# Graph products of an attention kernel gathered in one block: order of products, denominators and keys

## The chip, the cores and the metric

The kernel runs on one core of one Trainium2 chip. The metric is the device time of one execution in microseconds; three runs of the kernel before took 2455.43, 2456.01 and 2456.99 us, median 2456.01. Below, PE is the matmul engine, ACT the engine for activations and copies, DVE the vector engine, POOL the second, slower vector engine, SP the engine whose queue issues most DMAs. L1066 is line 1066 of the kernel before.

## The reference

Two layers over x (16 batches of 1024 nodes with 256 features, float32), each followed by a residual sum and a layernorm. The change touches the first layer only:

```python
c_adj = jnp.mean(fea, axis=1)                       # fea = x transposed, (B, C, N)
diff = c_adj[:, None, :] - c_adj[:, :, None]
A = jnp.abs(jnp.abs(jax.nn.sigmoid(diff) - 0.5) - 0.5) * 2.0
Wg = adj[None, :, :] * ((A + jnp.transpose(A, (0, 2, 1))) * 0.5)
g = jax.nn.relu(jnp.einsum('bcn,bnm->bcm', fea, Wg) * para.reshape(1, C, N))
q = ...   # g, cut into 4 heads of 64
k, v = ...  # x @ kv_w, cut likewise
out = jnp.einsum('bhnm,bhmd->bhnd', softmax(jnp.einsum('bhnd,bhmd->bhnm', q, k) * scale), v)
x = _layernorm(x + out)
```

The second layer multiplies with a normalised adjacency, then two linear maps with batchnorms, a residual and a layernorm.

## The kernel before, in words

**Stages.** The first layer runs batch by batch until about 1600 us of the span; the second layer follows in two passes over all batches. The first layer's instructions on PE, ACT, DVE and SP stand in exactly the order in which the program writes them (a manual schedule); POOL's follow in order as well. Buffers come from small pools: a tile takes a free buffer of its tag, and its first writer waits until the last reader of the buffer's former tile is done.

**Bursts.** The attention of a batch has 32 units: 2 pairs of heads, 2 halves of the queries, 8 chunks of the keys. Two units make a burst, 16 bursts (u = 0 to 15) make a batch. For a unit `scores` multiplies keys and queries into a PSUM tile of 1024 columns (`ps`, L1066, two buffers of tag "s"), and ACT takes the exponential into `p` (L1071, four buffers). `outputs` multiplies `p` with the values (`po`, L1087, two buffers of tag "o") and DVE adds `p` up into `acc` (L1095, L1097), the softmax's denominators still spread over partitions. In each turn of the loop PE gets the scores of burst j, then the outputs of burst j-1, and then whatever else stands at that u. When a half of the queries is complete, ACT and DVE bring the output out of PSUM (L1104, L1105), DVE transposes it in squares of 32 and SP sends it through memory (L1115, L1116, L1125).

**What else stands at which burst.** While batch b is attended to, batch b+1 is prepared and batch b-1 is finished:

- u=0: values and keys of batch b+1 (`steps`, seven of the eight, L1006 and L993), weights of its graph (`side`, L838, L843, L847), the denominators of the former batch's second pair (`normalise`, L1134: eight matmul passes with a matrix of ones, a copy `drow` on ACT L1140, four DMAs out and four in).
- u=1: `residual` of that pair (reciprocals L1155, POOL multiplies and adds, L1161 and L1162). u=2 and u=3: halves of the layernorm's statistics of batch b-1 on DVE (L620, L621); after the second, POOL makes the coefficients (L593, L595, L625, L626).
- u=4: two calls from `late`, `finish_x1` (L1180): eight blocks of `t * rstd + nmr` on ACT (L630), and after the second half the store of the result, issued by POOL (L1183).
- u=4 to u=8: the graph product of batch b+1, in seven block products of four accumulating steps each (eight matmul passes, `product`, L896) instead of eight, after Winograd. DVE makes the sums that they need: `left_first`, `left_third`, `left_last` of x (tile `S`), `right(1)` to `right(4)` of the weights (tile `wg`, in place, four subtractions each, L882). Products accumulate in PSUM tiles of tag "t" (two buffers); products 1 and 2 share `pga`, 3 has `pgd`, 6, 7 and 4 share `pgb`, 5 has `pgc`. Results are put together in `qT`, weighed with `para_s` and rectified (`weigh`, `rectify`).
- u=8: `begin` of batch b+2 (its column of means on DVE, L796, and five DMAs that spread it as a row), and `normalise` of the batch's own first pair. u=11: `residual` of that pair.
- u=9 to u=15: x of batch b+2 arrives in squares (L764) and is transposed by DVE (L820, u=12 and u=15); one step of its `side` per burst. In the last batch but one the adjacency's squares (L1249) come in the same places.

The part of the schedule that the change edits is, in the kernel before:

```python
elif u == 4:
    p = st[b + 1]["graph"]["p"]
    keys_last = steps[:1] if b else []
    del steps[: len(keys_last)]
    p[1]()
    run(keys_last, 1)
    run(late, 2)
    p[2]()
    p[3]()
```

Of the kernel before, what the change touches and what calls it, by code (L numbers as in the profile page):

```python
# [10 lines left out]
F32 = mybir.dt.float32  # L11
# [504 lines left out]
def fast_path(  # L516
# [43 lines left out]
    def tile_s(name):  # L560
        return psum["s"].tile([P, N], F32, tag="s", name=name)

    def tile_t(name):
        return psum["t"].tile([P, HALF], F32, tag="t", name=name)

    def tile_o(name):
        return psum["o"].tile([P, HALF], F32, tag="o", name=name)
# [167 lines left out]
    with (  # L735
# [46 lines left out]
        def prologue(b):  # L782
# [77 lines left out]
            KC = range(NCH // 2)  # L860

            def left_first():
                s2, s4 = s["S"][:, 0], s["S"][:, 1]
                nc.vector.tensor_tensor(s2, A21, A22, ALU.add)
                nc.vector.tensor_tensor(s2, s2, A11, ALU.subtract)
                nc.vector.tensor_tensor(s4, A12, s2, ALU.subtract)

            def left_third():
                nc.vector.tensor_tensor(s["S"][:, 1], A11, A21, ALU.subtract)

            def left_last():
                nc.vector.tensor_tensor(s["S"][:, 0], A21, A22, ALU.add)

            def right(k):
                for i in KC:
                    dst, one, two = {
                        1: (lo(i, H1), lo(i, H1), lo(i, H0)),
                        2: (hi(i, H1), hi(i, H1), lo(i, H1)),
                        3: (lo(i, H0), hi(i, H1), lo(i, H0)),
                        4: (hi(i, H0), hi(i, H0), hi(i, H1)),  # L880
                    }[k]
                    nc.vector.tensor_tensor(dst, one, two, ALU.subtract)  # L882
# [18 lines left out]
            def q_at(c, hs):  # L901
                return s["qT"][:, c, hs]

            def rectify(c, hs):
                q = q_at(c, hs)
                nc.scalar.activation(q, q, AF.Relu, scale=-scale)  # L906
# [4 lines left out]

            pg = {}

            def p1():
                s["qT"] = qkv.tile([P, CC, N], F32, tag="qT", name=f"qT_{b}")
                s["S"] = xsp.tile([P, 2, NCH // 2, P], F32, tag="xS", name=f"S_{b}")
                pg["a"] = tile_t(f"pga_{b}")
                product(1, pg["a"], True)
                nc.scalar.copy(q_at(1, H0), pg["a"])  # L919
                left_first()  # L920
                right(1)

            def p3():
                pg["d"] = tile_t(f"pgd_{b}")
                product(3, pg["d"], True)
                nc.scalar.copy(q_at(0, H1), pg["d"])

            def p2():
                product(2, pg["a"], False)
                nc.vector.tensor_mul(q_at(0, H0), pg["a"], para_s[:, 0, H0])  # L930
                rectify(0, H0)

            def between(u):
                right(u - 3)
                if u == 6:
                    nc.vector.tensor_add(q_at(0, H1), q_at(0, H1), q_at(1, H0))
                if u == 7:
                    left_third()

            def p6():  # L940
                pg["b"] = tile_t(f"pgb_{b}")
                product(6, pg["b"], True)
                nc.vector.tensor_add(q_at(0, H1), pg["b"], q_at(0, H1))
                left_last()

            def p7():
                product(7, pg["b"], False)
# [9 lines left out]

            def p4():
                product(4, pg["b"], False)
                nc.vector.tensor_add(q_at(1, H0), pg["b"], q_at(1, H0))  # L960
                weigh(1, H0)

# [78 lines left out]
                )]  # L1041
            if b:
                s["graph"] = dict(
                    between=between, p=(None, p1, p2, p3, p4, p5, p6, p7),
                )
            return first, steps, side

# [79 lines left out]
        def normalise(b, pr):  # L1127


            k = b * PAIRS + pr  # L1130
            last = k == B * PAIRS - 1
            den = tile_s("den_last")[:, H0] if last else tile_t(f"den_{k}")
            for i in range(4):
                nc.tensor.matmul(  # L1134
                    den[i * 32 : (i + 1) * 32, :], ones[:, :32],
                    G[b, pr, i // 2]["acc"][:, (i % 2) * HALF : (i % 2 + 1) * HALF],
                    start=True, stop=True,
                )
            row = rdp.tile([P, HALF], F32, tag="drow", name=f"drow_{k}")
            nc.scalar.copy(row, den)  # L1140
            for i in range(4):
                nc.sync.dma_start(den_d[k][i : i + 1, :], row[i * 32 : i * 32 + 1, :])
            for qh in range(2):
                col = small.tile([P, 4, 2], F32, tag="dcol", name=f"dcol_{k}_{qh}")
                for hd in range(2):
                    i = 2 * qh + hd
                    nc.sync.dma_start(
                        col[:, :, hd], den_d[k][i : i + 1, :].rearrange("o (n p) -> p (o n)", p=P)
                    )
                G[b, pr, qh]["col"] = col  # L1150
# [34 lines left out]
        def run(fs, k):  # L1185
            for f, a in fs[:k]:
                f(*a)
            del fs[:k]
# [135 lines left out]
        with tc.manual_schedule(  # L1324
# [64 lines left out]
            for j in range(len(bursts)):  # L1389
                b, u = j // PERB, j % PERB  # L1390
                for i in bursts[j]:
                    scores(i)
                if u == 0:
                    steps, side = next_steps, next_side
                    next_first, next_steps, next_side = [], [], []
                if j:
                    back(j - 1)
                if u in (5, 9, 13):
                    run(rows_of, 1)
                if u == 5 and b + 2 < B:  # L1400
                    load_x(b + 2)
                    next_first, next_steps, next_side = prologue(b + 2)
                if b == B - 1:
                    if u == 0:
                        run(sums, 1)
                        run(rows_of, 1)
                    elif u in (2, 13):
                        run(full, 2)
                    elif u == 8:
                        run(sums, 1)  # L1410
                    elif u == 3:
                        late.clear()
                elif u == 0:
                    for i in range(7):
                        if b:
                            run(steps, 1)
                            run(side, (2, 3, 2, 3, 2, 2, 99)[i])
                        if i == 1:
                            run(sums, 1)
                            run(rows_of, 1)  # L1420
                elif u < 4:
                    if u == 1:
                        run(full, 2)
                    else:
                        run(late, 1)
                    run(side, 99)
                elif u == 4:
                    p = st[b + 1]["graph"]["p"]
                    keys_last = steps[:1] if b else []
                    del steps[: len(keys_last)]  # L1430
                    p[1]()
                    run(keys_last, 1)
                    run(late, 2)
                    p[2]()
                    p[3]()
                elif u == 8:
                    p = st[b + 1]["graph"]["p"]
                    p[6]()
                    run(next_first, 1)
                    run(sums, 1)  # L1440
                    if b == B - 2:
                        adjacency_diagonal()
                        for n in range(6):
                            adjacency_rows(n)
                    p[7]()
                    p[5]()
                    p[4]()
                elif u < 8:
                    st[b + 1]["graph"]["between"](u)
                else:  # L1450
                    if u == 9 and b + 2 < B:
                        load_squares(b + 2, 0)
                    if u == 11:
                        run(full, 2)
                    if u == 12:
                        run(next_first, 1)
                        if b + 2 < B:
                            load_squares(b + 2, 1)
                    if u == 15:
                        run(next_first, 1)  # L1460
                    run(next_side, 1)
                if b == B - 2:
                    run(before_last.get(u, []), 9)
                if b == B - 1:
                    run(last.get(u, []), 9)
# [591 lines left out]
```

## Time and profile before

| what | value |
|---|---|
| median of three runs | 2456.01 us |
| profiled execution, its own time | 2458.24 us |
| its span, first to last instruction | 2456.5 us |
| PE busy | 2418.9 us, 98% |
| DVE busy | 1863.6 us, 76% |
| ACT busy | 1236.0 us, 50% |
| POOL busy | 478.5 us, 19% |
| mean granted clock of PE | 0.997 |
| one attention batch (281.27 to 377.96) | 96.69 us |

A line of a timeline has the start in us of the span, the length of the piece in us, engine, line, operation, what it writes and reads, shape and count; in brackets stands the idle time of that engine just before, and what ended it. A line of a table by stages has the stretch, its length, the busy time (and instructions) of PE, weight load, DVE, ACT and POOL, then the granted clock (1.00 is full), the share of the DMA engines and GB/s. The ends of matmuls are modelled, so PE's pace is read from starts.

### The profile page before, as it was taken

To read this page: it belongs to the slowest core of one execution; us is meant where nothing else is said; L and a number is where in the kernel's file an instruction comes from. 1 tells how busy PE (TensorE), PEld (TensorE's weight loads), DVE (VectorE), ACT (ScalarE), POOL (GpSimd) and SP (SyncE) were. 2 spreads that over 40 slices of the span, in tenths; PEclk is the share of its full clock that TensorE was granted. 3 is DMA by queue.
4 is the path that set the end of the run, shared out by engine and by line. 5 is a ranking of instruction groups with operands and counts; after the bars stand their busy time and mean duration, and the time that the engine had idled before them with its cause. 6 is when DMAs were issued, how large, how long until landed. Compare 5 with 4: busy or idle time off the path is not lost.

```text
span 2456.5 us, 32863 instructions
## 1 busy us (share of the span) xinstructions
PE 2418.9 (98%) x12446; PEld 1033.7 (42%) x12446; DVE 1863.6 (76%) x2572; ACT 1236.0 (50%) x1543; POOL 478.5 (19%) x487
## 2 busy tenths in 40 slices
PE   8999999999999999999999999999999999999997
PEld 4443443434434434434344343344444444444455
DVE  5678878888888788788888888855556556478978
ACT  6475665764765756657657667420111111145568
POOL 0021112211211211122112112522122122010026
PEclk9999999999999999999999999999999999999999
DMA  3123232232242333322322427221221222165559
GB/s 137 31 49 79 61 53 69 53 65 61 44 83 57 49 75 65 53 69 53 66 61 40 87 48 104 74 103 69 86 103 69 94 94 81 73 237 174 171 208 342
DMA packets 414648, 220.41 MB, mean 90 GB/s; under 512 B 353169, under 2 KB 386449, under 8 KB 406033
## 3 DMA queue, kind: packets, MB, share of 16 engines
q1 hardware_dynamic: 409120, 167.36, 27.9%
q0 software_dynamic: 4832, 50.34, 4.9%
q8 instruction: 99, 1.62, 0.3%
q14 instruction: 69, 0.56, 0.1%
q10 hardware_dynamic: 528, 0.52, 0.1%
HBM read 134.49 MB, written 83.69 MB: 89 GB/s over the span
## 4 chain that ended last, share of the span: by engine, by line
PE 84%; DVE 10%; ACT 3%; DMA 2%; issue 1%; SPq 0%; POOL 0%; POOLq 0%; DVEq 0%
PE ps L1066 17%; PE po L1087 17%; PE pgb L896 7%; PE b_agg L1564 4%; PE pga L896 4%; PE c_agg L1564 4%; PE pk L993 4%; PE b_o L1771 3%; PE pv L1006 2%; PE a_agg L1564 2%; PE b_h L1596 2%; PE pgc L896 2%; PE pgd L896 2%; PE c_o L1771 2%; PE a_o L1771 2%; PE c_h L1596 2%
## 5 line engine op out<-in xcount | busy, mean ns | idle before, releaser
L1071 ACT ACTIVATE p<-ps 128x1024 f32<-128x1024 f32 x512 | 497.1, 1021 | 182.5 <-PE ps L1066 123.8
L1097 DVE TENSOR_TENSOR acc<-acc,p 128x1024 f32<-128x1024 f32 x384 | 501.3, 1306 | 52.4 <-ACT p L1071 29.1
L1066 PE MATMUL ps<-qT,kT 64*64 64x512 f32 x4096 | 488.1, 592 | 0.3 <-ACT p L1071 0.3
L1087 PE MATMUL po<-p,v 64*64 64x512 f32 x4096 | 485.3, 589 | 0.0
L1161 POOL TENSOR_TENSOR o<-o,r_all 128x512 f32<-128x512 f32 x62 | 95.8, 1554 | 1106.5 <-DVE r_all L1155 1068.2
L1087 PEld LDWEIGHTS po<-p,v 64*64 64x64 f32 x4096 | 158.4, 133 | 281.0 <-issue 274.0
L1066 PEld LDWEIGHTS ps<-qT,kT 64*64 64x64 f32 x4096 | 151.5, 133 | 286.7 <-issue 249.4
L847 DVE SCALAR_TENSOR_TENSOR wg<-wg,adj_s 128x1024 f32<-128x1024 f32 x128 | 149.6, 1216 | 24.6 <-ACT wg L843 24.6
L838 ACT ACTIVATE wg<-crow,ccol 128x1024 f32<-128x1024 f32 x128 | 146.7, 1146 | 6.3 <-PE pg L978 6.1
L843 ACT ACTIVATE wg<-wg 128x1024 f32<-128x1024 f32 x128 | 135.9, 1062 | 0.9
L993 PE MATMUL pk<-xT,kvw_s 128*128 128x512 f32 x256 | 121.9, 598 | 3.1 <-ACT drow L1140 3.1
L1006 PE MATMUL pv<-kvw_s,xT 128*128 128x256 f32 x512 | 123.9, 385 | 0.0
L1006 PEld LDWEIGHTS pv<-kvw_s,xT 128*128 128x128 f32 x512 | 95.0, 190 | 50.2 <-issue 13.6
L906 ACT ACTIVATE qT<-qT 128x512 f32<-128x512 f32 x60 | 37.1, 626 | 149.8 <-DVE qT L909 145.3
L896 PE MATMUL pgb<-wg,S 128*128 128x512 f32 x240 | 111.0, 605 | 0.0
L896 PE MATMUL pga<-wg,x 128*128 128x512 f32 x240 | 109.6, 599 | 0.7 <-ACT qT L919 0.7
L1564 PE MATMUL a_agg<-ahT,x1l 128*128 128x512 f32 x240 | 108.1, 593 | 0.7 <-ACT agg L1312 0.7
L1564 PE MATMUL b_agg<-aT,x1S 128*128 128x512 f32 x240 | 107.9, 592 | 0.0
L1162 POOL TENSOR_TENSOR x<-x,o 128x512 f32<-128x512 f32 x62 | 106.9, 1735 | 2.4
L656 ACT COPY p_agg<-a_agg 128x512 f32<-128x512 f32 x15 | 8.8, 585 | 183.4 <-PE a_agg L1564 179.5
L692 POOL TENSOR_TENSOR x1S<-x1l 128x512 f32<-128x512 f32 x15 | 19.3, 1284 | 353.1 <-PE c_agg L1564 350.1
L1095 DVE TENSOR_TENSOR acc<-p,p 128x1024 f32<-128x1024 f32 x64 | 77.3, 1208 | 7.5 <-ACT p L1071 7.5
(234 smaller groups left out, 3522.0 us busy)
## 6 DMA issues: line engine op xcount, KB each, us to landing
h<-hw POOLq DMA_DIRECT2D x16, 2048.0 KB, 6.6
hl<-h SPq DMA_DIRECT2D x32, 1024.0 KB
x<-x POOLq DMA_DIRECT2D x16, 1024.0 KB, 4.3
x1l<-x SPq DMA_DIRECT2D x16, 1024.0 KB
xf<-x SPq DMA_DIRECT2D x16, 1024.0 KB
o<-oS SPq DMA_DIRECT2D x62, 256.0 KB
o<-o SPq DMA_DIRECT2D x248, 64.0 KB
x<-in_x_dram SPq DMA_DIRECT2D x15, 1024.0 KB
```

The source lines that it names most:

```text
L838: nc.scalar.activation(w, s["crow"], AF.Abs, bias=s["ccol"][:, n : n + 1])
L843: nc.scalar.activation(w, w, AF.Tanh, scale=0.5)
L847: nc.vector.scalar_tensor_tensor(w, w, 1.0, adj_s[:, n, :], op0=ALU.subtract, op1=ALU.mult)
L896: nc.tensor.matmul(ps, left, right, start=(start and i == 0), stop=(i == NCH // 2 - 1), skip_group_check=True,)
L993: nc.tensor.matmul(ps, kvw_s[:, c, kc * P : (kc + 1) * P], s["xT"][:, c, hs], start=(c == 0), stop=(c == CC - 1),)
L1006: nc.tensor.matmul(pt[:, j * C : (j + 1) * C], s["xT"][:, c, n * P : (n + 1) * P], kvw_s[:, c, C : 2 * C], start=(c == 0), stop=(c == CC - 1),
L1066: nc.tensor.matmul(ps[kh * D : (kh + 1) * D, hd * HALF : (hd + 1) * HALF], kT[r, pr, ks], qT[r, pr, qh * HALF : (qh + 1) * HALF], start=Tr ...
L1071: nc.scalar.activation(p, ps, AF.Exp)
L1087: nc.tensor.matmul(g["po"][kh][hd * D : (hd + 1) * D, :], s["v"][r, m, h * D : (h + 1) * D], p[r, hd * HALF : (hd + 1) * HALF], start=(m = ...
L1097: nc.vector.tensor_add(g["acc"], g["acc"], p)
L1564: nc.tensor.matmul(ps, left, right, start=(start and i == 0), stop=(i == NCH // 2 - 1), skip_group_check=True,)
L1771: nc.tensor.matmul(ps, left, right, start=(start and i == 0), stop=(i == 1), skip_group_check=True,)
```

## The change

The graph product's work at u=4 goes away. Its sums of x (`left_first`) are made at u=5, the first differences of the weights (`right(1)`) two at a time at u=6 and u=7, and all seven products stand at u=8, in the order 3, 1, 6, 2, 7, 5, 4; `right(2)`, `right(3)`, `right(4)`, `left_third` and `left_last` stand between them. The column of means of batch b+2 comes after product 6, as before. The denominators of the first pair move from between products 6 and 7 behind product 4, ahead of what DVE and ACT do with product 4 (`p4_out`), and take a buffer of tag "o" where they took one of tag "t". The eighth step of keys and values runs at u=0 with the other seven. At u=4 only the two calls of `finish_x1` are left.

```diff
+            def between(u):
+                if u == 5:
+                    left_first()
+                else:
+                    right(1, KC[2 * u - 12 : 2 * u - 10])
+
+            def p3():
+                s["qT"] = qkv.tile([P, CC, N], F32, tag="qT", name=f"qT_{b}")
+                pg["d"] = tile_t(f"pgd_{b}")
+                product(3, pg["d"], True)
+                nc.scalar.copy(q_at(0, H1), pg["d"])
+                right(2)
+                left_third()
+
             def p1():
-                s["qT"] = qkv.tile([P, CC, N], F32, tag="qT", name=f"qT_{b}")
-                s["S"] = xsp.tile([P, 2, NCH // 2, P], F32, tag="xS", name=f"S_{b}")
                 pg["a"] = tile_t(f"pga_{b}")
                 product(1, pg["a"], True)
                 nc.scalar.copy(q_at(1, H0), pg["a"])
-                left_first()
-                right(1)
...
+                right(3)
+                nc.vector.tensor_add(q_at(0, H1), q_at(0, H1), q_at(1, H0))
...
+            def p2():
+                product(2, pg["a"], False)
+                nc.vector.tensor_mul(q_at(0, H0), pg["a"], para_s[:, 0, H0])
+                rectify(0, H0)
+                right(4)
...
             def p4():
                 product(4, pg["b"], False)
+
+            def p4_out():
                 nc.vector.tensor_add(q_at(1, H0), pg["b"], q_at(1, H0))
                 weigh(1, H0)
...
-            den = tile_s("den_last")[:, H0] if last else tile_t(f"den_{k}")
+            if last:
+                den = tile_s("den_last")[:, H0]
+            elif pr == 0 and b < B - 1:
+                den = tile_o(f"den_{k}")
+            else:
+                den = tile_t(f"den_{k}")
...
-                    for i in range(7):
+                    for i in range(8):
                         if b:
                             run(steps, 1)
-                            run(side, (2, 3, 2, 3, 2, 2, 99)[i])
+                            run(side, (2, 3, 2, 3, 2, 2, 99, 0)[i])
...
                 elif u == 4:
-                    p = st[b + 1]["graph"]["p"]
-                    keys_last = steps[:1] if b else []
-                    del steps[: len(keys_last)]
-                    p[1]()
-                    run(keys_last, 1)
                     run(late, 2)
-                    p[2]()
-                    p[3]()
                 elif u == 8:
                     p = st[b + 1]["graph"]["p"]
-                    p[6]()
+                    for k in (3, 1, 6):
+                        p[k]()
                     run(next_first, 1)
-                    run(sums, 1)
                     if b == B - 2:
                         adjacency_diagonal()
                         for n in range(6):
                             adjacency_rows(n)
-                    p[7]()
-                    p[5]()
-                    p[4]()
+                    for k in (2, 7, 5, 4):
+                        p[k]()
+                    run(sums, 1)
+                    p[8]()
```

## The prediction

> **What bounds the kernel now.** I read the page's engine table first, then the sums of one attention batch, then the order of PE, ACT and POOL around the bursts that the change touches (the timelines of the fourth batch, b=3), and last the granted clock at the one place where PE rested for some microseconds.
>
> ```profile
> PE 2418.9 (98%) x12446; PEld 1033.7 (42%) x12446; DVE 1863.6 (76%) x2572; ACT 1236.0 (50%) x1543; POOL 478.5 (19%) x487
> ```
> ```profile
> 281.27:377.96 96.69, 96.47 (x636) 38.97 (x632) 79.71 (x104) 61.01 (x75) 18.34 (x13) 1.00 0.29 61
> 377.96:474.65 96.69, 96.46 (x636) 38.97 (x632) 79.73 (x104) 61.02 (x75) 18.35 (x13) 1.00 0.29 61
> ```
>
> PE bounds it (the columns after the window are span, then busy time of PE, weight load, DVE, ACT, POOL, then clock). A batch takes 96.69 us and PE rests 0.2 us of it. No edit that keeps every matmul can gain much; what it can do is open a hole in PE's work.
>
> ```profile
> 374.45 1.90 PE L1066 MATMUL ps<-qT,kT 64*64 64x512 f32 x16
> 376.16 1.90 PE L1087 MATMUL po<-p,v 64*64 64x512 f32 x16
> 377.99 3.70 PE L896 MATMUL pga<-wg,x 128*128 128x512 f32 x8
> 381.53 1.88 PE L993 MATMUL pk<-xT,kvw_s 128*128 128x512 f32 x4
> 383.25 3.60 PE L896 MATMUL pga<-wg,x 128*128 128x512 f32 x8
> 386.68 3.60 PE L896 MATMUL pgd<-wg,S 128*128 128x512 f32 x8
> 390.20 1.95 PE L1066 MATMUL ps<-qT,kT 64*64 64x512 f32 x16
> ```
> ```profile
> 378.36 0.58 ACT L1104 COPY oT<-po 128x512 f32<-128x512 f32 x1
> 381.73 0.59 ACT L919 COPY qT<-pga 128x512 f32<-128x512 f32 x1 [2.79 <-PE pga L896]
> 383.44 0.58 ACT L997 COPY kT<-pk 128x512 f32<-128x512 f32 x1 [1.13 <-PE pk L993]
> 384.70 4.04 ACT L630 ACTIVATE x<-x,nm_l,rs_l 128x256 f32<-128x256 f32 x8 [0.67 <-POOL nm_l L626]
> 388.65 0.61 ACT L906 ACTIVATE qT<-qT 128x512 f32<-128x512 f32 x1
> ```
> ```profile
> 379.57 1.11 POOL L593 TENSOR_SCALAR rs_l<-mv_l 128x8 f32<-128x8 f32 x1 [4.64 <-DVE mv_l L621]
> 380.76 2.68 POOL L595 TENSOR_TENSOR rs_l<-rs_l,mhalf 128x8 f32<-128x8 f32 x1
> 383.53 0.37 POOL L625 TENSOR_TENSOR nm_l<-mv_l,rs_l 128x8 f32<-128x8 f32 x1
> 383.99 0.68 POOL L626 TENSOR_SCALAR nm_l<-nm_l 128x8 f32<-128x8 f32 x1
> ```
>
> This is the fifth burst (u=4). PE does graph work from 377.99 to 390.20, and under it ACT does the eight row blocks of the previous batch's layernorm (L630): they wait until POOL has the coefficients, at 384.67, and end at 388.65. No exponential is due on ACT in those 12 us, so the wait costs nothing. That is the cover to watch.
>
> ```profile
> 2366.26 1.02 PE L1925 MATMUL pf<-ident,o 128*128 128x128 f32 x4 [2.98 <-ACT o L1901]
> ```
> ```profile
> 2360.00:2366.40 6.40, 3.42 (x10) 1.42 (x9) 2.64 (x7) 4.22 (x6) 0.55 (x1) 1.00 0.75 283
> 2366.40:2369.80 3.40, 3.40 (x17) 3.40 (x17) 2.63 (x6) 3.40 (x4) 0.00 (x0) 0.50 0.20 84
> ```
>
> Far from the change, a rest of 2.98 us on PE was followed by 3.4 us at a granted clock of 0.50.
>
> **The change, part by part.** *Fewer blocks of full-array products.* All matmuls stay. One slot is 3.43/8 = 0.429 us (383.25 to 386.68). The fifth burst's block takes 12.21 us for 28 slots = 12.00, plus 0.11 before it (the outputs at 376.16 take 1.83 against 1.72) and 0.05 after it (the scores at 390.20 take 1.77): 0.37 us of switching go, in 14 batches; batch 0 loses 1.3 there, because without keys its second product waits for the first copy. At the ninth burst the denominators split the block; it runs from 404.10 to 419.22, 15.12 us for 14.59 of work (32 slots and 0.86 of denominators), with 0.16 around it. Behind the last product one switch less remains: I take 0.2 us off in 15 batches, between 0 and 0.5. Sum: 14 x 0.37 + 1.3 + 15 x 0.2 = 9.5 us gained.
>
> *Keys in the first burst.* Two matmuls (four slots, 1.72 us) and a copy of 0.48 move; the copy falls before an exponential whose scores end later still. Cost nothing, but PE's second to fifth bursts start 1.72 us later against DVE and POOL.
>
> *The denominators.* In the ninth burst let S be the start of the next scores. Their copy runs at S+0.1 to 0.7 on ACT, behind two rectifications that DVE feeds before S-1.5; on SP they now stand behind the five issues of the column of means. Four issues of 0.29 and four of 0.5 bring the columns out by S+4.1 and in about 1.3 us later, as in the old order; the reciprocals read them at S+8.5 (331.00 against 322.53). Behind them in SP's queue the output squares leave by S+6.8 and the next x squares by S+9.2, landing 2 us later; DVE transposes them at S+16.0. In batch 14 the adjacency squares would come at S+11.1 against S+9.0: one DVE wait of 2.1 us, with four p buffers before PE notices. The denominators' buffer among the outputs' two is free at S+0.7, and the outputs want it at S+1.8. Cost nothing, with 3 us of margin at the closest.
>
> *The order of the products.* With T the first product's start, products follow at T+3.4, 6.9, 10.3, 13.7, 17.2, 20.6. DVE has about 22 us of work for these 25 (differences 12 x 0.60, sums and weighings 0.6 to 0.7 each, column of means 2.9, two accumulations 2.6, output and its transpose 1.4). Following its queue: second differences done at T+4.7, needed at 6.9; third at 7.8, needed at 13.7; fourth and the read of pgb at 18.5, needed at 20.6. Nothing stalls; the thinnest cover is 2.1 us. Were it gone, every microsecond of lateness would cost 15.
>
> *What is left at the fifth burst.* Only the eight layernorm blocks. They now stand on ACT directly between the output copy of the fifth burst and the exponentials of the sixth. Their coefficients hang on the reciprocals in the second burst (368.06), two POOL pairs, DVE's statistics (ended 379.47) and the four POOL rows above. None of it waits for the moved keys, so 384.67 stays. PE, 1.72 later: fifth scores 376.17, outputs 377.89, sixth scores 379.60, outputs 381.32, seventh scores due at 383.04. These need a score buffer; there are two, and both hold the sixth burst until ACT has read them. ACT: waits to 384.70, layernorm to 388.65, first exponential to 389.67 (one takes 1.02), 0.1 to signal: 389.8. PE waits 389.8 - 383.04 = 6.75 us. (The outputs at 381.32 also wait, for an output buffer that DVE frees at 382.51; that lies inside the same hole.) Behind the layernorm POOL stores x (389.04) and SP loads the next x into the freed buffer; the column of means reads it in the ninth burst, some 22 us later, where it had 20. DVE's first sums of the graph need less than the hole. It happens for every batch that has a predecessor and a successor: 14 x 6.75 = 94.5 us.
>
> *The clock after the hole.* Nothing before shows it here. From below: no drop, 0. From the row above: 3.4 us at half clock cost 1.7; twice that, 3.4, if the hole drops the clock and the next stretch does not restore it. PE's unbroken rest is about 5.6 us (384.2 to 389.8), longer than the 2.98 that sufficed there, so I lean to the row: 1.7 in 8 of 10 holes, 14 x 0.8 x 1.7 = 19 us (ends 0 and 48).
>
> The Trainium skill, "TensorE: Matmul & The Clock Gate", section "Part 1: The HAM clock gate", halves the clock after a whole idle window of about 3.4 us on a free-running grid, and its section "Why this matters for your kernels" warns of rests over about 3 us. The row agrees with the second; by the first, 5.6 us holds a whole window in 64% of cases, an estimate from that page, and the term would be 15 us.
>
> **Sum.** -9.5 + 94.5 + 19 = +104 us. The profiled execution took 2458.24 (span 2456.5), the median of the runs shown is 2456.01; I add to the median: 2560.
>
> **The rivals.** *Faster: the layernorm stays hidden.* If ACT were free for the sixth burst's exponential in time, only the 9.5 us remain: 2446.5. For it: the queues carry the same work, and ACT is half idle. Against it: the blocks would have to start by 378.0, 6.7 us before POOL has ended. It decides below that point.
>
> *Hole without the clock.* As forecast but at full clock throughout: 2456 - 9.5 + 94.5 = 2541. For it: other short waits (0.7 us) left the clock at 1.00; against it: the row at 2366.
>
> *DVE late in the ninth burst, or the clock low for two stretches.* Lateness of 1 to 2 us over the 2.1 margin would add 15 to 30, the second stretch up to 29: 2575 to 2590 and somewhat over. For it: DVE's row of slices stands at 8 through the attention; against it: the queue above, and the hole itself lets DVE catch up.
>
> *A smaller hole*, 1 to 5 us, if the coefficients come earlier: 14 x 1 to 5 less 9.5, 2461 to 2516. POOL's first pair took 1.98 and 2.13 against 1.04 and 1.27 for its second, so 2 us of play exist at most.
>
> **How the numbers follow.** Forecast 0.60 (2548 to 2575), no clock drop 0.15, later DVE or longer drop 0.13, smaller hole 0.04, hidden 0.07, no change 0.01. The range 2530 to 2590 holds the first two and half of the third: 0.82. A difference of 0.2%, 4.9 us, is about what a measurement here can tell from none; by the cases: faster 0.07, same 0.01, slower 0.92.
>
> **What would show it.** Right: in the batches' waits a new group, PE scores waiting for exponentials (p, L1071) some 6 to 7 us at a time, 14 times; ACT waiting for nm_l some 4 us at a time; a batch span of about 104 us; half clock in many batches just after the hole; no wait inside the ninth burst's block. Wrong: layernorm blocks that start before 378, or PE waiting for DVE differences. What would break the forecast is a coefficient chain that moves with PE, since then the hole shifts with its terms.

## The result, and the profile after

The changed kernel takes 2584.63 us (median of four runs, 2583.22 to 2586.30) against 2455.86 us for the kernel before: a ratio of 1.0523, 95% interval 1.0507 to 1.0538. It is about 129 us slower. The forecast was 2560 with a range of 2530 to 2590; direction and mechanism came out, the price was 25 us too low. The time lies outside the band of the forecast itself (2548 to 2575, chance 0.60) and inside that of the rival "DVE late in the ninth burst, or the clock low for two stretches" (2575 to 2590, chance 0.13); of that rival it was the clock. The profiled execution took 2583.67 us, its span is 2581.8, so in the profiles 125.3 us of span are to be explained.

The engine table of the kernel after, PE's line (busy time, share of the span, instructions):

```profile
PE 2461.7 (95%) x12446; PEld 1042.8 (40%) x12446; DVE 1864.7 (72%) x2572; ACT 1239.9 (48%) x1543; POOL 482.2 (19%) x487
```

The instructions of PE are as many as before, and yet its busy time rose by 43 us and its share fell: it both rests more and runs slower. Two batches of the kernel after, an early and a late one, by stages (length, then busy PE, weight load, DVE, ACT and POOL, granted clock, DMA share, GB/s), cut where the seventh burst's scores start:

```profile
404.41:509.94 105.53, 99.46 (x633) 39.67 (x633) 79.86 (x104) 61.28 (x75) 18.78 (x13) 0.97 0.27 56
1356.16:1461.98 105.82, 99.75 (x633) 39.69 (x633) 79.87 (x104) 61.28 (x75) 18.78 (x13) 0.97 0.28 56
```

A batch was 96.69 us and is now up to 105.82; PE rests some 6 us of it, and its mean clock is 0.97 where it was 1.00. The place is the fifth to seventh bursts. PE's timeline there, kernel after:

```profile
390.45 1.90 PE L1070 MATMUL ps<-qT,kT 64*64 64x512 f32 x16
392.17 1.90 PE L1091 MATMUL po<-p,v 64*64 64x512 f32 x16
393.89 1.90 PE L1070 MATMUL ps<-qT,kT 64*64 64x512 f32 x16
395.60 1.02 PE L1091 MATMUL po<-p,v 64*64 64x512 f32 x2
396.86 1.94 PE L1091 MATMUL po<-p,v 64*64 64x512 f32 x14 [0.24 <-DVE oT L1109]
404.41 1.13 PE L1070 MATMUL ps<-qT,kT 64*64 64x512 f32 x4 [5.61 <-ACT p L1075]
```

ACT's timeline in the same stretch:

```profile
394.12 0.59 ACT L1108 COPY oT<-po 128x512 f32<-128x512 f32 x1 [0.62 <-PE po L1091]
399.41 4.04 ACT L630 ACTIVATE x<-x,nm_l,rs_l 128x256 f32<-128x256 f32 x8 [4.71 <-POOL nm_l L626]
403.36 1.91 ACT L1075 ACTIVATE p<-ps 128x1024 f32<-128x1024 f32 x2
```

And POOL's, which makes the coefficients:

```profile
393.86 1.11 POOL L593 TENSOR_SCALAR rs_l<-mv_l 128x8 f32<-128x8 f32 x1 [4.64 <-DVE mv_l L621]
395.06 2.68 POOL L595 TENSOR_TENSOR rs_l<-rs_l,mhalf 128x8 f32<-128x8 f32 x1
397.82 0.91 POOL L625 TENSOR_TENSOR nm_l<-mv_l,rs_l 128x8 f32<-128x8 f32 x1
398.82 0.56 POOL L626 TENSOR_SCALAR nm_l<-nm_l 128x8 f32<-128x8 f32 x1
```

The three are read together. The eight layernorm blocks stand ahead of the sixth burst's exponential in ACT's queue; they wait 4.71 us for POOL, run for 3.95, and the exponential follows at 403.36. Its result lets the seventh scores start at 404.41. Without a rest they would have started at 390.45 + 6.87 = 397.32 (four blocks at 1.72): 7.09 us are lost. In the waits of the kernel after, this is a new group on PE that the kernel before had at 0.3 us in all, with its cause on ACT (total, times, longest; 14 of PE's 15 are the holes, the other is a wait of 0.28 us near the start):

```profile
PE ps L1070 <- ACT p L1075: 78.7, 15, 5.6
```
```profile
ACT x L630 <- POOL nm_l L626: 62.2, 14, 4.7
```

The clock answers. The same place in windows of 3.41 us, cut where the granted clock (the column after POOL) changes:

```profile
398.78:402.20 3.42, 0.02 (x3) 0.00 (x0) 1.88 (x3) 2.79 (x6) 0.56 (x1) 1.00 0.17 49
402.20:405.61 3.41, 1.20 (x8) 0.55 (x12) 1.22 (x1) 3.07 (x5) 0.65 (x1) 0.50 0.64 154
405.61:409.02 3.41, 3.41 (x20) 0.97 (x16) 3.31 (x5) 1.81 (x2) 0.00 (x0) 0.50 0.54 221
409.02:412.44 3.42, 3.42 (x36) 1.13 (x32) 2.82 (x5) 1.41 (x3) 0.00 (x0) 1.00 0.91 289
```

PE was idle in the first window, and two windows at half clock follow it, not one: the first of them is two thirds rest, and only after the second, which PE filled, is the clock full again. PE worked 4.6 us at half pace (20 matmuls in the second low window, where the window at full clock has 36); that cost 2.3 us here.

Because the scores are the same 4096 matmuls in the same order in both kernels, their starts give the bookkeeping. Start after less start before, in us, for the first scores of some bursts (worked out from the two traces):

```
batch   burst 1   burst 4   burst 6   burst 7   burst 9   burst 10  burst 16
  0      -0.82     -0.82    -12.37    -12.42    -12.42     -2.32     -2.32
  1      -2.32     -0.60    -12.93     -5.88     -4.38      5.72      5.72
  3      14.29     16.01      3.68     10.72     13.04     23.13     23.13
 13     104.93    106.64     94.32    101.36    103.95    114.05    114.05
 14     114.05    115.76    103.44    110.48    113.08    123.17    124.68
 15     124.68    125.51    125.52    125.91    125.91    126.51    126.51
```

From burst 6 to 7 comes the rest (+7.04 with 0.05 of the switching gained), from 7 to 9 the clock (+1.50 in batch 1, 2.32 in batch 3, 2.6 from batch 8 on). The moved work itself nearly cancels: +1.72 for the keys, -12.33 at the fifth burst, +10.1 at the ninth.

### The profile page after: what moved, and what is told of

Read it like the earlier page. It is cut to its first block, busy times and chain, and to the rows that moved or that the text cites. A ratio compares the mean times of both kernels' runs of the same rounds, so it can differ in the third digit from the quotient of the medians.

```text
span 2581.8 us, 32820 instructions
## 1 busy us (share of the span) xinstructions
PE 2461.7 (95%) x12446; PEld 1042.8 (40%) x12446; DVE 1864.7 (72%) x2572; ACT 1239.9 (48%) x1543; POOL 482.2 (19%) x487
## 5 line engine op out<-in xcount | busy, mean ns | idle before, releaser
L1070 PE MATMUL ps<-qT,kT 64*64 64x512 f32 x4096 | 516.9, 617 | 78.7 <-ACT p L1075 78.7
L1091 PE MATMUL po<-p,v 64*64 64x512 f32 x4096 | 516.8, 600 | 4.9 <-DVE oT L1109 4.9
L1091 PEld LDWEIGHTS po<-p,v 64*64 64x64 f32 x4096 | 164.8, 136 | 318.1 <-issue 292.2
L1109 DVE TENSOR_TENSOR oT<-po,oT 128x512 f32<-128x512 f32 x64 | 44.1, 690 | 92.1 <-ACT oT L1108 92.1
L630 ACT ACTIVATE x<-x,nm_l,rs_l 128x256 f32<-128x256 f32 x128 | 64.8, 588 | 66.9 <-POOL nm_l L626 62.2
```

What stands on the lines that cost most here:

```text
L1070: nc.tensor.matmul(ps[kh * D : (kh + 1) * D, hd * HALF : (hd + 1) * HALF], kT[r, pr, ks], qT[r, pr, qh * HALF : (qh + 1) * HALF], start=Tr ...
L1091: nc.tensor.matmul(g["po"][kh][hd * D : (hd + 1) * D, :], s["v"][r, m, h * D : (h + 1) * D], p[r, hd * HALF : (hd + 1) * HALF], start=(m = ...
```

## The experiments

Two theories stood at first. Mine: the lost cover. The blocks wait for POOL on ACT ahead of an exponential; the clock adds to it. Rival: the ninth burst, where all products, their DVE work and the denominators now stand close together, costs a good part. All ratios below are to the kernel before on the same chip.

**The blocks where they disturb nobody (after, blocks spread over bursts 7 to 9).**

```diff
-                        for f in (statistics_x1, finish_x1):
-                            for ns in (range(NCH // 2), range(NCH // 2, NCH)):
-                                late.append((f, (b, ns)))
+                        for ns in (range(NCH // 2), range(NCH // 2, NCH)):
+                            late.append((statistics_x1, (b, ns)))
+                        for ns in (range(3), range(3, 6), range(6, NCH)):
+                            late.append((finish_x1, (b, ns)))
...
                 elif u == 4:
-                    run(late, 2)
+                    pass
...
                 elif u == 8:
                     p = st[b + 1]["graph"]["p"]
+                    run(late, 1)
...
                     st[b + 1]["graph"]["between"](u)
+                    if u > 5:
+                        run(late, 1)
```

> The changed kernel with the eight layernorm blocks taken from the fifth burst and spread over the seventh (3), eighth (3) and ninth (2), behind their exponentials. Theory (the blocks in front of the sixth burst's exponentials make the hole, the hole lowers the clock): no wait of 5.6 us, no half clock, a batch of about 96.1 us, 2447 to 2449 us, a little faster than before. Rival (products in one block cost the time themselves, by DVE's differences or the buffers): the batch stays near 105 us and the time near 2580.

Measured: 2468.78 us, ratio 1.0044 (1.0030 to 1.0058); clock 0.998. The hole and every half-clock stretch of the attention are gone, so some 118 of the 129 us hang on where these blocks stand. But the 2447 to 2449 that I expected was missed by about 20. A batch takes 97.45 us, and PE still waits in each at the sixth burst. PE's and DVE's timelines there, this kernel:

```profile
380.14 1.02 PE L1091 MATMUL po<-p,v 64*64 64x512 f32 x2
381.40 1.51 PE L1091 MATMUL po<-p,v 64*64 64x512 f32 x11 [0.25 <-DVE oT L1109]
```
```profile
376.09 0.42 DVE L620 BATCH_NORM_STATS2 st_l<-x 128x6 f32<-128x256 f32 x1
...
378.23 2.52 DVE L1101 TENSOR_TENSOR acc<-acc,p 128x1024 f32<-128x1024 f32 x2
380.67 0.68 DVE L1109 TENSOR_TENSOR oT<-po,oT 128x512 f32<-128x512 f32 x1
```

The outputs of the fifth burst need the buffer that DVE's L1109 empties, at 381.35, and DVE comes late to it because the second half of the layernorm's statistics (376.09 to 378.31) stands ahead. With the graph products at the fifth burst, as in the kernel before, PE had 12 us of other work here. That is the wait which the prediction had seen as lying "inside the same hole": it does, and it shows when the hole is closed. From the two outputs at 380.14 to the product at 393.57 there are 112 matmuls of 0.107, so 12.0 of the 13.4 us; 1.3 us, net of 0.1 for a switch, are lost per batch.

**No wait for the coefficients (after, blocks with constants).** This kernel leaves out the layernorm's scale and shift.

```diff
-                    bias=nmr[:, n : n + 1], scale=rstd[:, n : n + 1],
+                    bias=mhalf[:, n : n + 1], scale=mhalf[:, n : n + 1],
```

> The changed kernel, with the eight blocks at their place in the fifth burst but with scale and bias from a constant column, so that they don't wait for POOL's coefficients (the layernorm's scale and shift of the first layer are left out for 14 batches; another product of the same size stands for them). Theory: ACT's wait of 4.7 us goes, 3.95 us of blocks remain, of which some 2.4 us reach PE; that is too short for the clock gate, so 14 x 2.4 = 33 us over the hole-free kernel: about 2480 at full clock. Rival (the blocks' own work is what counts, not the wait): near 2585 still. Rival (clock falls for this hole too): 2500 or more.

Measured: 2484.80 us, ratio 1.0107 (1.0092 to 1.0123); full clock in the attention. In the waits of this kernel the group on PE shrinks from 78.7 to 11.4 us:

```profile
PE ps L1070 <- ACT p L1075: 11.4, 15, 0.8
```

The blocks' own 4 us on ACT cost little; what makes the hole is that they stand waiting for POOL in an in-order queue. The time came out 5 us above the expected 2480, and the batch of 98.52 us is 1.07 above that of the spread blocks, where with the wait it was up to 8.4 above: a wait of 0.80 is still there. That a rest of 2.4 us would leave the clock full, as the expectation had it, was not tested, since the rests ahead of the seventh scores are 0.8 here.

**How the price goes with the size of the hole (after, seven or four blocks at the fifth burst, the rest at the seventh).** The edit for seven; for four both sevens are fours:

```diff
+                        for ns in (range(7), range(7, NCH)):
+                            late.append((finish_x1, (b, ns)))
...
                 elif u == 4:
-                    run(late, 2)
+                    run(late, 1)
...
                     st[b + 1]["graph"]["between"](u)
+                    if u == 6:
+                        run(late, 1)
```

> The changed kernel with seven blocks in the fifth burst and the eighth behind the seventh burst's exponentials: the hole's cause is 0.49 us shorter in 14 batches. Theory of the grid (half clock ends on a fixed grid of 3.413 us, so the batch locks to 31 windows = 105.81 us, and a shorter hole is given back as a longer stretch at half clock): batch still 105.81, time within 2 us of 2584.6. Linear rival: 14 x 0.49 = 7 us less, 2577.7, or 10 us less if the stretch at half clock shrinks with it.

> The changed kernel with four blocks in the fifth burst and four in the seventh: the hole's cause is 1.98 us shorter. Linear rival: 14 x 1.98 = 28 us less, 2557. Theory of the grid: 31 windows would need 9.1 us at half clock per batch, more than the two windows seen, so the batch cannot stay at 105.81; 30 windows, 102.40 us, would need 2.3 us at half clock: 2537 to 2540 if so short a stretch ends at the window's edge, or batches of both lengths in turn, between 2540 and 2580.

Seven: 2580.23 us, ratio 1.0496 (1.0481 to 1.0510), unbroken rests of 5.12 us in place of 5.61. Four: 2549.60, ratio 1.0373 (1.0358 to 1.0389), rests of 3.64. Where the seventh bursts' scores start, the distances from hole to hole are, in us:

```
after  104.73 105.26 105.52 105.68 105.74 105.79 105.79 105.81 105.81 105.81 105.80 105.82 105.82
seven  104.49 105.24 105.52 105.67 105.75 105.78 105.79 105.80 104.10 104.97 105.37 105.60 105.72
four   103.06 103.01 103.01 102.71 104.25 103.02 103.01 102.72 104.25 103.02 103.01 102.73 104.26
```

A rest shorter by 0.49 us changed the batch by nothing: it too runs up to 105.8, which is 31 windows of 3.4133 us (105.81). Only at the ninth distance does it slip, and the run is 3.2 us of span shorter than the kernel after, where 14 x 0.49 = 6.9 had come off the rests; PE's work at half pace cost 37.0 us there against 33.9. My expectation of at most 2 us missed that slip. The time alone does not decide against the linear rival's 7 us (the ratio is 0.27% lower than that of the kernel after, with intervals of 0.15% either way); the distances do. What happens at it is one window; the kernel with seven, first a hole where the half clock lasts two windows, then the slip:

```profile
931.62:935.03 3.41, 2.69 (x16) 0.87 (x20) 2.61 (x3) 2.17 (x3) 0.00 (x0) 0.50 0.13 23
935.03:938.45 3.42, 3.42 (x24) 0.99 (x20) 3.32 (x4) 1.95 (x3) 0.48 (x1) 0.50 0.01 2
...
1037.43:1040.85 3.42, 2.71 (x16) 0.89 (x20) 2.62 (x3) 2.17 (x3) 0.00 (x0) 0.50 0.09 14
1040.85:1044.26 3.41, 3.41 (x40) 1.14 (x36) 3.31 (x4) 2.13 (x4) 0.65 (x1) 1.00 0.02 5
```

2.69 us of PE's work in the first low window were not enough to bring the full clock back, 2.71 were. So the clock goes by whole windows, and it comes back behind a window that was busy for at least about 0.79 of its time. In the kernel with four blocks three holes of four cost one low window and the fourth costs two, in a steady pattern. Its profiled execution is 34.7 us under that of the kernel after (2548.95 against 2583.67): 14 x (5.61 - 3.64) = 27.6 are rest, the other 7 clock (27.0 against 33.9 us lost at half pace). Of what had been expected, the linear rival's 2557 and the 2537 to 2540 of an even 30 windows both missed; the time lies between 2540 and 2580, as it had been put for batches of two lengths in turn.

**One more block on ACT (after, a ninth block ahead of the eight, or behind them).** If the batch is held to 31 windows, a rest half a microsecond longer must not lengthen it either. The first edit put the block ahead:

```diff
+        junk = const.tile([P, C], F32, name="junk")
...
                 elif u == 4:
+                    if late:
+                        nc.scalar.activation(
+                            junk, st[b - 1]["x"][:, 0, :], AF.Identity,
+                            bias=mhalf[:, 0:1], scale=mhalf[:, 0:1],
+                        )
                     run(late, 2)
```

> The changed kernel with a ninth block of the same size ahead of the eight (into an unused buffer): the hole's cause is 0.49 us longer. Grid (3.413 us windows; full clock is lost when PE is busy for less than about 0.41 of a window, regained at about 0.79): batches start near 106.6 us and come down to 105.81 by halves (106.2, 106.0, 105.9, ...), 4 us more than the changed kernel in all, ratio 1.054. Linear rival: every batch 0.49 us longer, 106.3 without a trend, 7 us more, ratio 1.055; the lengths of the batches tell them apart.

Measured: 2584.52 us, ratio 1.0516 (1.0500 to 1.0532), rests of 5.60: the block ran inside ACT's wait for POOL, so the edit did not lengthen the hole and settles nothing. Behind the eight it does:

```diff
+        junk = const.tile([P, C], F32, name="junk")
...
                 elif u == 4:
+                    xt = st[b - 1]["x"] if late else None
                     run(late, 2)
+                    if xt is not None:
+                        nc.scalar.activation(
+                            junk, xt[:, 0, :], AF.Identity,
+                            bias=mhalf[:, 0:1], scale=mhalf[:, 0:1],
+                        )
```

> The changed kernel with a ninth block of the same size behind the eight (into an unused buffer), which e7_nine had put into ACT's wait, where it cost nothing: now PE's rest must be 6.1 us. Grid with two thresholds: batches begin above 105.81 us (106.7, 106.2, 106.0) and come down to it by halves; 4 us more than the changed kernel. Linear rival: all batches 0.49 us longer than the changed kernel's, 106.3 at the end, 7 us more.

Measured: 2586.65 us, ratio 1.0528 (1.0512 to 1.0544), rests of 6.10. One early and two late batches of it:

```profile
300.69:406.77 106.08, 99.50 (x632) 39.69 (x632) 79.87 (x104) 61.85 (x76) 18.82 (x13) 0.97 0.25 56
1253.54:1359.34 105.80, 99.24 (x632) 39.59 (x632) 79.86 (x104) 61.79 (x76) 18.79 (x13) 0.97 0.27 56
1359.34:1465.15 105.81, 99.24 (x632) 39.59 (x632) 79.86 (x104) 61.78 (x76) 18.80 (x13) 0.97 0.27 56
```

The kernel after came up to 105.81 from 104.73; this one comes down to it from 106.35, and the late batches are as long as those of the kernel after, though the rest is 0.49 longer. With a clock term that doesn't depend on the phase they would be 106.3. The half-clock time that PE works through fell from 2.58 to 2.08 us' worth per hole: the longer rest is paid back, microsecond for microsecond, by time at half clock. The span is 2.1 us longer, not 6.9, and nearer to the lock's forecast than to the other.

**The keys alone (before, the eighth step of the keys at the first burst).**

```diff
-                    for i in range(7):
+                    for i in range(8):
...
-                    keys_last = steps[:1] if b else []
-                    del steps[: len(keys_last)]
                     p[1]()
-                    run(keys_last, 1)
                     run(late, 2)
```

> The kernel before with one part of the change alone: the eighth step of keys and values stands in the first burst. Graph products and layernorm blocks stay at the fifth. Theory: no hole, because 10.3 us of products still cover the blocks; product 2 now waits for the copy of product 1, 0.7 us as batch 0 showed it, in 14 batches: 10 us more, ratio 1.004. Rival (keys moved past the output buffers open the hole): a wait of several us per batch, ratio 1.03 or more.

Measured: 2470.75 us, ratio 1.0056 (1.0040 to 1.0071), a batch of 97.64 against 96.69. PE's timeline at its fifth burst:

```profile
380.04 3.70 PE L896 MATMUL pga<-wg,x 128*128 128x512 f32 x8
384.41 3.70 PE L896 MATMUL pga<-wg,x 128*128 128x512 f32 x8 [0.68 <-ACT qT L919]
```

The keys filled the time in which ACT copies the first product out of the buffer that the second one accumulates in. The idle time is shown as 0.68 us, but it starts at a modelled end; by the starts, 384.41 - 380.04 less the 3.43 of eight passes, 0.94 us are lost. Taken alone, the step costs 0.95 us a batch, 13 us in 14 batches, where 10 were expected; it is harmless in the whole change because another product stands between products 1 and 2 there. There is no hole here: ACT's blocks still lie under the products.

**Removing what was left (spread blocks, and the statistics one burst later).** If the statistics ahead of L1109 cause the wait of the first experiment, a later place for them ends it. The blocks now stand in the eighth burst (three) and the ninth (five); the edit is to the kernel with the spread blocks.

```diff
-                        for ns in (range(3), range(3, 6), range(6, NCH)):
+                        for ns in (range(3), range(3, NCH)):
...
-                    else:
+                    elif u == 3:
                         run(late, 1)
...
                 elif u == 4:
-                    pass
+                    run(late, 1)
...
-                    if u > 5:
+                    if u == 7:
                         run(late, 1)
```

> As e1_spread, but DVE's statistics of the former batch stand one burst later (first half in the fourth, second in the fifth burst, behind the output's sum), and the blocks in the eighth (3) and ninth (5) burst. Theory: the 1.3 us that PE loses per batch in e1_spread are the outputs of the fifth burst waiting for the buffer that DVE's output sum frees late because the statistics stand before it; they go, a batch takes 96.1 to 96.3 us, the time is 7 to 9 us below the kernel before (ratio 0.996 to 0.997). Rival (the shorter cover at the fifth burst costs for another reason): the batch stays at 97.4 us, ratio 1.004.

Measured: 2459.17 us, ratio 1.0007 (0.9998 to 1.0017). The wait for the output buffer is gone, which shows its cause; but the blocks end later, so x is stored later and its buffer is loaded later, and the column of means waits for it. DVE's and PE's timelines of this kernel:

```profile
309.00 2.29 DVE L796 TENSOR_REDUCE csum<-x 128x8 f32<-128x2048 f32 x1 [2.66 <-DMA x<-in_x_dram]
```
```profile
312.44 3.70 PE L897 MATMUL pgc<-wg,S 128*128 128x512 f32 x8 [0.83 <-DVE qT L944]
```

2.66 us of wait on DVE, 0.83 on PE: the ninth burst's cover on DVE is about as thin as forecast (2.1), and here it is used up. Batches take 96.2 to 97.3, and the expected ratio of 0.996 to 0.997 was missed.

**The place of the denominators, and of the column of means.** Three kernels, all on the last one: the denominators back between products 6 and 2; the column of means later, behind product 7; and both.

```diff
                     run(next_first, 1)
+                    run(sums, 1)
...
-                    for k in (2, 7, 5, 4):
+                    for k in (2, 7, 5, 4, 8):
                         p[k]()
-                    run(sums, 1)
-                    p[8]()
```

> As e8_stats, with the first pair's denominators back between products 6 and 2 (still in a buffer of tag o). Theory: one more switch between full-array products and the denominators' 32 columns, 0.2 us a batch, 15 batches: 3 us more than e8_stats. Rival (place makes no difference): within 1 us.

```diff
-                    run(next_first, 1)
...
-                    for k in (2, 7, 5, 4):
+                    for k in (2, 7):
+                        p[k]()
+                    run(next_first, 1)
+                    for k in (5, 4):
                         p[k]()
                     run(sums, 1)
```

> As e8_stats, with the column of means (DVE, L796) behind product 7 instead of product 6. Theory: in e8_stats this column waited for x (loaded late, because the layernorm's store is late) and kept DVE's differences from products 5 and 4; behind product 7 the load is in time, no product waits, a batch takes 96.15 us, ratio 0.996 to 0.997. Rival (block with the denominators at its end is too tight for DVE anyway): the batch stays over 96.5 us, ratio 0.999 to 1.001.

```diff
                     for k in (3, 1, 6):
                         p[k]()
+                    run(sums, 1)
...
-                    run(sums, 1)
                     p[8]()
```

> As e10_means, with the first pair's denominators back between products 6 and 2. With no product waiting in either, this is the price of their place: 0.26 us a batch (96.42 against 96.15), 4 us over 15 batches, less about 1.3 us in the last batch but one, whose adjacency squares come in time again: 2 to 3 us more than e10_means. Rival (place makes no difference): within 1 us.

Measured: denominators back 2453.07 us, ratio 0.9985 (0.9976 to 0.9994); means later 2452.53, ratio 0.9979 (0.9970 to 0.9988); both 2453.36, ratio 0.9983 (0.9974 to 0.9992). The first was expected to lose 3 us against the kernel with later statistics and gained 6 (2453.07 against 2459.17): its column of means still waits for x, 1.8 to 2.8 us in 13 batches, but the denominators between the products give DVE 1 us more, and PE no longer felt it. The second has the lowest ratio of this study, 0.21% under the kernel before, though the intervals of the three overlap. One batch of "means later" and one of "both":

```profile
390.30:486.52 96.22, 96.00 (x637) 39.20 (x633) 81.20 (x104) 61.09 (x75) 20.75 (x13) 1.00 0.30 61
```
```profile
391.47:487.89 96.42, 96.20 (x636) 39.11 (x633) 81.28 (x104) 61.06 (x75) 20.75 (x13) 1.00 0.30 61
```

So the denominators behind the last product are worth 0.20 us a batch. But in the last batch but one that place costs. DVE and PE there, "means later":

```profile
1487.65 1.25 DVE L1262 STREAM_TRANSPOSE ahT<-aS 128x1024 f32<-128x1024 f32 x1 [5.25 <-DMA aS<-in_adj_dram]
```
```profile
1491.99 1.51 PE L1091 MATMUL po<-p,v 64*64 64x512 f32 x11 [1.50 <-DVE oT L1109]
```

and DVE in the kernel with both, where no wait stands before the same instruction:

```profile
1487.38 1.19 DVE L1262 STREAM_TRANSPOSE ahT<-aS 128x1024 f32<-128x1024 f32 x1
```

With the denominators early the adjacency's squares are there in time; with them late DVE waits 5.25 us and PE, through the output buffer, 1.50. Over the whole kernel the two places come out within 1 us of each other (2452.53 and 2453.36), where 2 to 3 had been expected. In the profiles the kernel with both is 4.4 us behind "means later" ahead of that place, 0.9 of it by one wait in batch 11, and 2.1 behind at the last scores.

## Why the prediction was right or wrong

**The hole: right, with a size 5% off.** Place, cause, waiting engine and count (14) are as forecast. The prediction had 6.75 us, and it is 7.09. POOL's four rows took 5.52 us from start to end where they took 5.10 before (L625 0.91 against 0.37), so the coefficients came 0.43 later against PE, and the signal to PE was 0.10 shorter than put in: 6.75 + 0.43 - 0.10 = 7.08. Why L625 took longer is not shown. Sum 14 x 7.09 = 99.3 against 94.5.

**The clock: the mis-sized term, 19 forecast, 34 measured.** The step that failed is the size "1.7 in 8 of 10 holes". All 14 holes dropped the clock, and 13 of the 14 for two windows. PE's working time at half pace, halved, is 1.5, 2.0, 2.3, 2.4, 2.5 and then 2.6 us per hole, together 34. The prediction named this as its upper case ("twice that, 3.4, if the hole drops the clock and the next stretch does not restore it") and leaned to the other by the one row that it had, at 2366.26 us, where PE came back at a window's start. Here the rests ended inside the first low window, and in 13 holes PE was busy for only 0.18 to 0.51 of it, too little to restore the clock; in the first hole it was 0.87, and one window was all. That the time still fell into the stated range owes to the range's upper end, which had been set for such cases, and not to the term. The Trainium skill, "TensorE: Matmul & The Clock Gate", section "Part 1: The HAM clock gate", asks for a whole idle window before the clock halves; the traces here disagree, since in the kernel with four blocks all 14 rests of 3.64 us halved it, and in none of them was the window ahead of the drop wholly idle: PE was busy for 0.02 to 0.39 of it. The first of the 14, the window ahead of the drop and the one behind it:

```profile
190.29:193.70 3.41, 1.34 (x12) 0.41 (x16) 1.60 (x3) 3.06 (x6) 0.00 (x0) 1.00 0.49 77
193.70:197.12 3.42, 3.42 (x20) 1.07 (x16) 3.42 (x4) 3.02 (x5) 0.00 (x0) 0.50 0.01 2
```

The page's free-running grid of 3413 ns agrees with the 105.81 = 31 windows.

**Fewer blocks: right.** 0.37 + 0.2 us a batch were forecast, 0.55 came: by the table of starts a batch without its hole and clock gains -12.33 + 1.72 + 10.10 - 0.05 = -0.56, and the denominators' part is 0.20 by the pair of kernels above. Batch 0 gained 1.5 in its two blocks (-0.82 to -2.32), forecast 1.3 + 0.2; the -0.82 arose before any changed place.

**Keys: right in the whole change.** They cost nothing but 1.72 us of delay. That rests on the order of the products: alone the step costs 0.95 us a batch.

**Denominators: wrong in batch 14.** "One DVE wait of 2.1 us, with four p buffers before PE notices" failed. DVE waited 5.04 us in the kernel after:

```profile
1619.48 1.25 DVE L1262 STREAM_TRANSPOSE ahT<-aS 128x1024 f32<-128x1024 f32 x1 [5.04 <-DMA aS<-in_adj_dram]
```

PE noticed, not through p but through the output buffer which DVE empties behind the waiting transpose: +1.51 in batch 14, and +1.83 more in batch 15, where the lateness goes on (which of its waits hangs on what was not separated). In the other batches the margin held: no wait, as forecast.

**The ninth burst: right.** No product waits inside its block. The thin cover was there, as the kernel with later statistics shows.

**The output buffer: seen, but wrongly free in a rival.** It lies in the hole, as said. But the rival "the layernorm stays hidden", 2446.5, forgot that it then shows, at 1.3 us a batch: the kernel with the spread blocks, which is that rival made real, took 2468.78.

Summed: 99.3 (holes) + 34 (clock) - 14 x 0.55 - 1.5 - 0.8 (start) + 1.5 + 1.8 = 126.6, against 126.51 us by which the last scores start later.

## What to carry to other kernels

When a block of work is moved, look first at what ran under it on the other engines: the products were moved for a gain of half a microsecond a batch, and the eight activations which they had covered were left alone in an in-order queue, waiting for POOL ahead of work that PE needs. The cheap repair is to move the covered work along with its cover, and then to ask again who came late to what; here that took two more small moves (the statistics, then the column of means or the denominators) before a gain of 0.2% showed. And a rest of some microseconds on PE has a second price, paid in whole windows of the clock, which can be a third of the first.

## What the runs showed of the hardware

**The clock goes by the busy share of a window, with two bounds.** The traces of all thirteen kernels were cut into the windows of 3.413 us at whose edges the granted clock changes, from 60 us of the span on, and PE's pieces (whose ends are modelled) added up in each. Every window at full clock that was busy for up to about 0.41 of its time was followed by half clock, and from 0.42 on none but one was. At half clock, every window busy for 0.793 or more brought the full clock back, and none up to 0.789 did. The closest pair at the lower bound, from the ends of two kernels. The kernel after, a window with 1.39 us of work and what follows it:

```profile
2566.23:2569.64 3.41, 1.39 (x10) 0.96 (x8) 3.17 (x14) 1.26 (x4) 2.68 (x6) 1.00 1.01 332
2569.64:2573.06 3.42, 0.00 (x0) 0.00 (x0) 3.21 (x15) 2.24 (x5) 2.38 (x5) 0.50 0.68 231
```

The kernel with a ninth block behind, 1.44 us, after which the clock stays full for one more window, in which PE does nothing, and only then falls:

```profile
2568.40:2571.82 3.42, 1.44 (x10) 1.01 (x8) 3.18 (x14) 1.28 (x4) 2.71 (x6) 1.00 1.01 331
2571.82:2575.23 3.41, 0.00 (x0) 0.00 (x0) 3.20 (x15) 2.30 (x5) 2.40 (x4) 1.00 0.67 231
```

The one exception is in the kernel with a ninth block ahead, where PE waits 1.54 us for an output buffer; the window is busy for 0.55 and half clock follows. Why is open:

```profile
1621.86:1625.28 3.42, 1.88 (x18) 0.42 (x13) 3.28 (x5) 1.65 (x2) 0.00 (x0) 1.00 1.42 137
1625.28:1628.69 3.41, 3.41 (x20) 1.07 (x24) 3.41 (x4) 1.43 (x3) 0.54 (x1) 0.50 1.08 144
```

By the lower bound, as an estimate, a rest of about 2 us (0.59 of 3.413) is enough if it falls into one window; waits of 0.8 to 1.5 us left the clock full in the experiments with spread blocks and with constants.

**A loop with a hole locks to the grid.** Every microsecond by which PE comes back later within the low windows is a microsecond less at half clock, so half of the deviation from a whole number of windows is gone a batch later: the distances of the kernel after fall short of 105.81 by 1.08, 0.55, 0.29, 0.13, 0.07, and those of the kernel with a ninth block behind exceed it by 0.54, 0.27, 0.13, 0.05. While it is locked, half a microsecond more or less in the hole doesn't show in the time.
